# A three-layer graph network and a token FFN on one core: the pace at which gathered sets are added in layers 2 and 3

## The chip, the cores and the metric

The kernel runs on one core of one Trainium2 chip. The metric is the device time of one execution in microseconds (us); lower is better. A core has five engines that run side by side and meet at semaphores: TensorE (PE in the profile; PEld is its weight load), VectorE (DVE), ScalarE (ACT), GpSimd (POOL) and SyncE (SP), which here only issues DMAs.

## The reference, cut to what matters

Inputs: `x` (6250 nodes x 256), 200,000 edges `src -> dst` (sorted by `dst`), three 256x256 weights, and an FFN.

```python
def conv(x, W, b):                      # one layer, with self loops
    h = x @ W
    return segment_sum(h[src] * norm[:, None], dst) + b

h = relu(conv(layernorm(x), W1, b1))
h = relu(conv(h, W2, b2))
x = x + conv(h, W3, b3)
# then a gated FFN on the 3124 nodes with the highest router weight, taken by top_k
```

`norm` is `dinv[src] * dinv[dst]`. So each layer sums, for every node, the rows of its neighbours. The edge count per destination falls with the node's number.

## The kernel before, in words

The 6250 nodes make 49 tiles of 128 rows. The sum over neighbours is done in two ways, both on TensorE:

- **By counts** (tiles 0 to 30, `DENSE = 31`): a dense matrix of edge counts is built once in layer 1, kept in DRAM (`counts`), and multiplied with all source rows (`hl`, each row as a float32r value and its remainder, so 512 columns). A tile takes 49 matmuls. They come in 7 *steps* of 7 matmuls (`add_up`, L735). Each step needs a *piece* of 7 x 128 counts: loaded by SP (`whole`, L932), eight loads ahead, and cast to float32r by `piece_of`, on ACT (L727) or, for the piece numbers in `CASTS`, on DVE (L729): numbers 0 and 3 in layer 2, number 3 in layer 3. Casts run two steps ahead (`AHEAD`).
- **Gathered** (tiles 31 to 48): their edges are cut into 359 *chunks* of 128 edges, two chunks to a *set*, so `SETS` is 180. For a chunk POOL fetches the source rows by an indirect DMA (`fetch`, L600). ACT and DVE split the rows of a set into value and remainder and DVE makes a selection matrix (`halve`, L609 and L619; `rest`, L624). TensorE adds it with two matmuls (`add_set`, L632). A gathered tile ends with one matmul for its own rows (L637). Up to seven sets are fetched ahead (`MSGS`).

In layers 2 and 3 the loop over `order` (L942 to L973) has 217 steps: 14 for tiles 0 and 1, whose pieces alternate, and 7 for each of tiles 2 to 30. In each step `prepare` halves the sets that the *next* step will add and casts the piece for two steps on, `add_up` does the 7 matmuls, and `gathered` adds the sets that are due. How many are due after step k is the list `now["due"]`, made by `pace`:

```python
def pace(n, late):
    return [max(0, SETS * (k + 1 - late)) // (n - late) for k in range(n)] + [SETS] * 2
```

`LATE[1]` is 6. With n = 217 the 180 sets fall on steps 7 to 216, 0 or 1 to a step, so about every seventh step has no set, and the last set of tile 48 is added in step 216, the last step of tile 30.

A finished tile goes through `onward`, which hangs its later work on the ends and starts of later steps (`at_end`, `at_start`), so that it stands in each engine's order among that step's work:

- `total` (DVE, L527 and L528), at the end of the next step. In layers 1 and 2: `turned` (PE transposes, L287), `positive` (ACT, L293), `multiplied` (PE, L298), `sent_on` (ACT, L545, and a DMA to `sent`, L546).
- In layer 3 `total` goes on to `residual` (DVE, L549 to L555), which adds the input row tile. SP loads that tile (`c_xt`, L522) when `onward` is called; for tile 48, which is not full, DVE zeroes it first (L521). Then `rooted` (ACT, L560), `normalised` (DVE, L276 to L281 and L568 to L576) and `summed` (ACT, L581, and DMAs to `c_rows` and `out`, L582 and L583), each at the end of one step later.

PE, DVE, ACT and POOL run in the order written here; the order on SP's queue comes from the scheduler. After the loop `finish` runs what is still hung up. The next layer starts by reading `sent` back (`arrive`, L950 to L952); POOL can gather for it only when all of `sent` has landed. After layer 3 the top-k search begins (L1012 on), and its L1017 waits for the last DMAs out of layer 3's buffers.

Of the kernel before, what the change touches and what calls it, by code (L numbers as in the profile page):

```python
# [56 lines left out]
LATE = [12, 6]  # L57
# [50 lines left out]
def by_counts(  # L108
# [396 lines left out]
    def next_step():  # L505
        run(1)
        steps.append(None)
        run(0)

    def finish():  # L510
        while behind:
            next_step()


    def onward(layer, t, pa):
        xt = None
        if layer == 2:
            n = P if t < NT - 1 else LAST
            xt = later["2"].tile([P, D], FP, name="c_xt2", bufs=4)
            if n < P:  # L520
                nc.vector.memset(xt[96:, :], 0.0)  # L521
            nc.sync.dma_start(xt[:n, :], x[t * P : t * P + n, :])  # L522
        at_end(1, total, layer, t, pa, xt)
# [62 lines left out]
    SETS = ceil(len(CHUNKS) / GB)  # L586
# [64 lines left out]
    def gathered(layer, now, until):  # L651
        for b in range(now["added"], until):
            add_set(layer, b)
        now["added"] = max(now["added"], until)
# [69 lines left out]
    def piece_of(layer, counts_7, i):  # L724
        piece = later["l3"].tile([P, PIECE, P], FR, name="piece")
        if layer is None or i not in CASTS[layer]:
            nc.scalar.activation(piece, counts_7, AF.Copy)  # L727
        else:
            nc.vector.tensor_copy(piece, counts_7)  # L729
        return piece  # L730

    def add_up(pa, piece, i, parts, sources=range(NT // PIECE)):
        for j in parts:
            q = i * PIECE + j
            nc.tensor.matmul(  # L735
                pa, piece[:, j, :], hl[:, q].rearrange("p two d -> p (two d)"),
                start=(i == sources[0] and j == 0), stop=(i == sources[-1] and j == PIECE - 1),
            )

    def new_sums():  # L740
        return ps_a.tile([P, 2 * D], FP, name="c_pa")

    NS = NT // PIECE
    AHEAD = 2

    def pace(n, late):

        return [max(0, SETS * (k + 1 - late)) // (n - late) for k in range(n)] + [SETS] * 2

    def prepare(layer, now, n, order, cast):  # L750

        made = ready(layer, now, now["due"][n + 1]) if n >= LATE[layer > 0] - 5 else []
        if n + AHEAD < len(order):
            cast(n + AHEAD)
        for m in made:
            if m:
                rest(*m)
# [65 lines left out]
    now = {"fetched": 0, "halved": 0, "added": 0}  # L823
# [3 lines left out]
    order = [(t, i) for t in TILES_BY for i in range(NS)]  # L827
# [9 lines left out]
    def cast(n):  # L837
        t, i = order[n]
        pieces[n] = piece_of(0 if n < len(order) - 2 * NS else None, strips[t][:, i * PIECE : (i + 1) * PIECE, :], i)
# [90 lines left out]
    def load(t, i):  # L930
        whole = l8p.tile([P, PIECE, P], F16, name="whole")
        nc.sync.dma_start(  # L932
            whole.rearrange("p h d -> p (h d)"), counts[t][:, i * PIECE * P : (i + 1) * PIECE * P]
        )
        return whole

    with tc.manual_schedule(engines=ordered):
        for layer in (1, 2):
            now = {"fetched": 0, "halved": 0, "added": 0}
            pieces = {}  # L940

            sources = SOURCES[layer - 1]  # L942
            order = [(t, i) for i in sources for t in range(2)]
            order += [(t, i) for t in range(2, DENSE) for i in range(NS)]
            now["due"] = pace(len(order), LATE[1])

            def arrive(i):
                for q in range(i * PIECE, (i + 1) * PIECE):
                    m = l8p.tile([P, D], FP, name="message")
                    nc.sync.dma_start(m, sent[layer][q * P : (q + 1) * P, :])  # L950
                    nc.scalar.activation(hl[:, q, 0, :], m, AF.Copy)
                    nc.vector.tensor_sub(hl[:, q, 1, :], m, hl[:, q, 0, :].bitcast(FP))  # L952

            def cast(n):
                t, i = order[n]
                pieces[n] = piece_of(layer, load(t, i), i)

            for n in range(AHEAD):
                cast(n)
            arrive(sources[0])  # L960
            sums = {}
            for n, (t, i) in enumerate(order):
                prepare(layer, now, n, order, cast)
                by = sources if t < 2 else range(NS)
                if i == by[0]:
                    sums[t] = new_sums()
                if t == 0 and i != sources[-1]:
                    arrive(sources[sources.index(i) + 1])
                add_up(sums[t], pieces.pop(n), i, range(PIECE), by)
                gathered(layer, now, now["due"][n])  # L970
                if i == by[-1]:
                    onward(layer, t, sums.pop(t))
                next_step()  # L973
            finish()
# [727 lines left out]
```

## Time and profile before

| | |
|---|---|
| median of 7 runs | 2401.84 us (2395.0 to 2417.58) |
| the profiled execution: its time | 2402.01 us |
| its span, first to last instruction | 2400.2 us, mean granted TensorE clock 0.931 |
| busy over the span | PE 1995.5, PEld 1498.7, DVE 1367.7, ACT 1207.8, POOL 1251.4 us |
| 943 to 1535 us (layer 2) | PE 524.2, DVE 284.0, ACT 294.3, POOL 361.3 of 592 us |
| 1584 to 2136 us (layer 3 after its start) | PE 457.1, DVE 386.6, ACT 282.7, POOL 335.7 of 552 us |

The profile is one execution. Its times run from the span's start. A line such as `2129.16 4.29 DMA c_xt<-in_x` in the chain of waits says: from 2129.16 us on, for 4.29 us, what came next waited for that transfer. In a timeline the bracket at the end of a line gives the engine's idle time before the instruction and what ended it. Matmul rows overlap, so their weight loads (PEld) show the pace better: seven loads of a step take 1.57 us at full clock.

### The profile page before, as it was taken

The page shows a single profiled execution, that of the slowest core. Times are in us where ns is not written, and L with a number is a line of the kernel's source. Part 1 is how long each engine was busy: PE and PEld are TensorE (multiplying, and loading weights), DVE is VectorE, ACT ScalarE, POOL GpSimd, SP SyncE. Part 2 cuts the span into 40 slices and gives each one's busy share as a digit, 9 for nine tenths or more (in the row PEclk, how much of TensorE's full clock was granted, in tenths as well). Part 3 has the DMA queues.
Part 4 walks back from the last instruction along what each step waited for, and adds up shares of the span by engine and source line. Part 5 has one row for each costly group of instructions (what it writes and reads, how often), then busy time and mean ns, then how long its engine had stood idle before and what let it go on. Part 6 is the DMA issues. An engine that isn't in the chain of part 4 may idle for free.

```text
span 2400.2 us, 30448 instructions
## 1 busy us (share of the span) xinstructions
PE 1995.5 (83%) x9636; PEld 1498.7 (62%) x9636; DVE 1367.7 (57%) x3370; ACT 1207.8 (50%) x1986; POOL 1251.4 (52%) x1228
## 2 busy tenths in 40 slices
PE   4849899989998876888989889888888878845997
PEld 2636666666676655666777677666666656634665
DVE  6475555666677784644444444477676767763111
ACT  2667677655656433644544544565454545431111
POOL 5325666666665501555666566466656656611221
PEclk8859999999999988999999999999999999976999
DMA  6276788787876514865666556587676767731110
GB/s 187 81 256 196 211 250 249 220 246 232 231 234 195 174 52 140 258 182 177 185 176 189 175 178 181 179 266 214 200 211 210 217 202 227 210 103 42 48 54 22
DMA packets 229052, 435.60 MB, mean 181 GB/s; under 512 B 35358, under 2 KB 139092, under 8 KB 224881
## 3 DMA queue, kind: packets, MB, share of 16 engines
q0 software_dynamic: 92992, 205.70, 30.5%
q1 hardware_dynamic: 104357, 192.11, 25.0%
q10 hardware_dynamic: 31532, 35.75, 4.4%
q8 instruction: 78, 1.28, 0.2%
q14 instruction: 93, 0.76, 0.1%
HBM read 335.50 MB, written 99.61 MB: 181 GB/s over the span
## 4 chain that ended last, share of the span: by engine, by line
PE 55%; DVE 17%; issue 8%; ACT 7%; another core or an unknown queue 5%; DMA 3%; POOL 3%; ACTq 1%; SPq 0%; DVEq 0%; POOLq 0%
PE c_pa L735 27%; PE ps_g L632 8%; PE ps_b L689 5%; PE c_ph L1135 4%; PE c_po L1143 4%; PE c_pt L298 4%; DVE half L624 3%; POOL msg L600 3%; ACT strip L705 2%; ACT piece L727 2%; PE ps_x L298 2%; DVE hot_l L669 2%; DVE hot_w L669 2%; ACT half L619 1%
## 5 line engine op out<-in xcount | busy, mean ns | idle before, releaser
L735 PE MATMUL c_pa<-hl,piece 128*128 128x512 f32 x4557 | 1301.2, 418 | 62.7 <-ACT piece L727 25.1
L735 PEld LDWEIGHTS c_pa<-hl,piece 128*128 128x128 f32 x4557 | 855.0, 197 | 247.1 <-issue 44.8
L600 POOL DMA_INDIRECT msg<-sent,source x718 | 722.0, 1006 | 537.3 <-DVE half L624 211.1
L600 POOL DMA_INDIRECT half<-sent,source x359 | 384.3, 1070 | 251.8 <-PE ps_g L632 81.9
L609 DVE TENSOR_TENSOR pick_sel<-up_h,local 128x256 fp32r<-128x256 f16 x540 | 227.4, 421 | 433.9 <-PE ps_g L632 210.9
L632 PE MATMUL ps_g<-half,pick_sel 128*128 128x512 f32 x1077 | 358.7, 412 | 98.4 <-DVE half L624 90.0
L727 ACT ACTIVATE piece<-whole 128x896 fp32r<-128x896 f16 x341 | 320.0, 941 | 157.3 <-remote 58.4
L705 ACT ACTIVATE strip<-ps_b 128x441 f16<-128x441 f32 (+3 forms) x441 | 304.1, 750 | 184.5 <-PE ps_b L689 144.4
L619 ACT ACTIVATE half<-msg 128x512 fp32r<-128x512 f32 x360 | 223.8, 625 | 294.8 <-PE ps_g L632 81.6
L632 PEld LDWEIGHTS ps_g<-half,pick_sel 128*128 128x128 f32 x1077 | 201.5, 194 | 174.6 <-DVE half L624 119.3
L624 DVE TENSOR_TENSOR half<-msg,half 128x512 fp32r<-128x512 f32 x360 | 248.5, 690 | 87.3 <-ACT half L619 48.8
L689 PE MATMUL ps_b<-hot_w,hot_l 128*128 128x98 f16 (+2 forms) x2171 | 213.9, 225 | 96.8 <-DVE hot_l L669 47.1
L689 PEld LDWEIGHTS <-hot_l 128*128 128x128 f16 x2171 | 139.0, 101 | 216.0 <-issue 148.3
L727 ACT ACTIVATE piece<-strip 128x896 fp32r<-128x896 f16 x159 | 150.7, 949 | 99.8 <-PE c_pa L735 78.9
L669 DVE TENSOR_TENSOR hot_w<-up_w,codes 128x1176 f16<-128x1176 f16 (+2 forms) x181 | 165.6, 915 | 61.3 <-PE ps_b L689 46.7
L669 DVE TENSOR_TENSOR hot_l<-up_l,codes 128x1536 f16<-128x1536 f16 x181 | 172.4, 952 | 0.0
L1139 ACT ACTIVATE ht<-c_ph,b_sb 128x512 f32<-128x512 f32 (+2 forms) x64 | 38.0, 594 | 188.4 <-PE c_ph L1135 185.7
L298 PE MATMUL c_pt<-c_wg,c_zt 128*128 128x256 f32 x392 | 102.9, 388 | 6.5 <-ACT c_zt L293 4.7
L1151 POOL DMA_INDIRECT out<-o,pick x25 | 25.2, 1007 | 140.6 <-DVE o L1148 140.6
L1147 DVE TENSOR_TENSOR o<-c_po,b_sb 128x256 f32<-128x256 f32 x25 | 10.6, 425 | 149.2 <-PE c_po L1143 149.2
L1135 PE MATMUL c_ph<-yt,w_sb 128*128 128x512 f32 (+2 forms) x256 | 91.1, 515 | 0.6 <-DVE yt L1130 0.6
L1143 PE MATMUL c_po<-w_sb,ht 128*128 128x256 f32 x400 | 88.5, 381 | 0.0
(218 smaller groups left out, 1561.3 us busy)
## 6 DMA issues: line engine op xcount, KB each, us to landing
whole<-counts SPq DMA_DIRECT2D x434, 224.0 KB
counts<-strip SPq DMA_DIRECT2D x31, 1568.0 KB
c_rows<-ys ACTq DMA_DIRECT2D x49, 256.5 KB
sent<-hl SPq DMA_DIRECT2D x7, 1792.0 KB
sent<-c_h ACTq DMA_DIRECT2D x98, 128.0 KB
message<-sent SPq DMA_DIRECT2D x98, 128.0 KB
msg<-sent,source POOLq DMA_INDIRECT x718
c_xt<-in_x SPq DMA_DIRECT2D x48, 128.0 KB
```

What stands on the lines that cost most here:

```text
L298: nc.tensor.matmul(pt[:, 1, :], zt[:, k, :], w_sb[:, k, :], start=(k == 0), stop=(k == KD - 1))
L600: nc.gpsimd.indirect_dma_start(out=out_j, out_offset=None, in_=sent[layer], in_offset=bass.IndirectOffsetOnAxis(ap=source[:, i : i + 1], a ...
L609: nc.vector.tensor_tensor(pick[:, :n], up_h[:, None, :].to_broadcast([P, n, P]), local[:, b * GB : b * GB + n, None].to_broadcast([P, n, P ...
L619: nc.scalar.activation(half[:, :n, 0, :], msg[:, :n], AF.Copy)
L624: nc.vector.tensor_sub(half[:, :n, 1, :], msg[:, :n], half[:, :n, 0, :].bitcast(FP))
L632: nc.tensor.matmul(open_sums[t], pick[:, j, :], half[:, j].rearrange("p two d -> p (two d)"), start=(k == 0), stop=False)
L669: nc.vector.tensor_tensor(rows_k[:, : n // 2, :cols, :], up[:, None, :cols, :].to_broadcast([P, n // 2, cols, 2]), code.rearrange("p (k tw ...
L689: nc.tensor.matmul(pb[:, at_c : at_c + NT * width], row_l[:, k // 2, :, k % 2], row_w[:, k // 2, : NT * width, k % 2], start=(c == 0), sto ...
L705: nc.scalar.activation(strip[:, :, d0 : d0 + n * width].rearrange("p h (a j) -> p a h j", j=width), pb[:, at_c : at_c + n * NT * width].re ...
L727: nc.scalar.activation(piece, counts_7, AF.Copy)
L735: nc.tensor.matmul(pa, piece[:, j, :], hl[:, q].rearrange("p two d -> p (two d)"), start=(i == sources[0] and j == 0), stop=(i == sources[ ...
L1135: nc.tensor.matmul(ph[:, : n * P], w1_sb[:, k, f * P : (f + 1) * P], yt[:, k, : n * P], start=(k == 0), stop=(k == KD - 1),)
```

## The change

In layers 2 and 3 the pace is computed for 7 steps fewer (`NS` is 7), and the last 7 steps get the full number.

```diff
             order += [(t, i) for t in range(2, DENSE) for i in range(NS)]
-            now["due"] = pace(len(order), LATE[1])
+
+            now["due"] = pace(len(order) - NS, LATE[1]) + [SETS] * NS
```

With n = 210 the 180 sets fall on steps 7 to 209, and steps 210 to 216, which are tile 30, add none. Steps 12 to 210 held 30 steps without a set; now steps 14 to 201 hold 23. Tile 48 ends in step 209, which is also the last step of tile 29. Nothing is added or removed otherwise, and the lines from L946 on move down by one.

## The prediction

> **What bounds the kernel now.** I read the page first, to see which engine carries the span. In the chain that ended last TensorE has the largest share:
>
> ```profile
> PE 55%; DVE 17%; issue 8%; ACT 7%; another core or an unknown queue 5%; DMA 3%; POOL 3%; ACTq 1%; SPq 0%; DVEq 0%; POOLq 0%
> ```
>
> The change moves matmuls within layers 2 and 3 and adds none, so what counts is where TensorE idles there. Second view: PE's waits, for layer 2 (943 to 1541 us) and then layer 3 (1541 to 2140 us); columns: total us, times, longest.
>
> ```profile
> PE ps_g L632 <- DVE half L624: 35.2, 22, 3.7
> ...
> PE ps_g L632 <- DVE half L624: 54.7, 35, 3.9
> PE c_pa L735 <- ACT piece L727: 17.8, 5, 5.8
> ```
>
> The reader is to see that the largest wait is a set's matmuls waiting for their remainder from DVE: 1.6 us each (35.2 / 22, 54.7 / 35), in a layer of 600 us. POOL is not the bound: 361.3 us busy of 592 in layer 2, and its last gather begins at 1517.8, when six more sets are still to be added.
>
> Third view: the ends of the two layers in the chain of waits (start, us, what). First layer 2, where tiles 48 and 30 end together:
>
> ```profile
> 1534.28 1.60 PE c_pa L735 x7
> 1535.88 0.23 PE ps_g L632
> 1536.11 0.25 PE ps_g L637
> 1536.38 0.49 DVE c_z L527
> ...
> 1538.44 0.41 PE c_pt L287 x2
> 1538.86 0.88 PE c_pt L298 x4
> ...
> 1540.69 0.48 ACT c_h L545
> ```
>
> The reader is to see PE end its sums at 1536.36 and the second tile's last ACT operation begin 4.33 us later. Layer 3:
>
> ```profile
> 2128.86 0.28 DVE c_xt L521
> 2129.16 4.29 DMA c_xt<-in_x
> ...
> 2133.55 0.43 DVE c_z L549
> ...
> 2139.35 0.08 DVE c_rstd L276
> ...
> 2141.90 3.35 DMA out<-ys
> ...
> 2145.37 0.15 DVE bits L1017
> ```
>
> Here PE's sums end at 2131.6 (L637 in the timeline). Everything up to 2145.37 is DVE, ACT and DMA for the two tiles, one after the other: 13.8 us in which PE has two matmuls of 1 column. Fourth view, the stretches of the last seven steps (us, then busy us of PE and PEld with counts):
>
> ```profile
> 1520.00:1536.36 16.36, 16.34 (x74) 13.17 (x72) 7.07 (x14) 7.30 (x13) 0.00 (x0) 1.00 0.45 124
> ...
> 2114.50:2131.60 17.10, 14.69 (x63) 11.32 (x61) 12.75 (x47) 8.15 (x14) 0.00 (x0) 1.00 0.15 53
> ```
>
> In layer 2 they have no gap; in layer 3 PE idles 2.4 us, before the set added at 2122.54.
>
> **The change, part by part.** *Units.* A step's seven matmuls take 1.60 us, a set 0.47, a tile's way through L287 and L298 0.22 + 0.87 = 1.09 (rows at 1524.05 and 1524.27 of the same chain). No instruction is added, so the sum starts at 0 and takes only waits and overlap.
>
> *Work moved off the last seven steps.* Six sets and L637 of tile 48 (6 x 0.47 + 0.25 = 3.1 us of PE) stand earlier in each layer. PE does them either way: 0.
>
> *End of layer 2.* Tile 48 now ends in step 209, and its 1.09 us on PE run inside steps 210 to 216 instead of after them: the sums end 1.09 later. Then one tile is left, and its L545 begins 3.16 us after PE's last sum, as at the end of layer 1, where tile 0 ends alone (sum ends 936.63, L545 at 939.79): 4.33 - 3.16 = 1.17 saved. Net **-0.1**. What follows (two casts, the first rows of layer 3, POOL's first gather) hangs on that same store in both. Between -1.2 (if the 1.09 falls into a gap) and +1.1 (if the single tile gains nothing).
>
> *End of layer 3.* One tile alone: from its own rows, L527 (2134.76) to the end of L555 (2137.07) 2.31, the root on ACT and the way back 0.3, L276 to the issue of the last store 2.64 (2139.26 to 2141.90), landing 3.35, L1017 0.1: 8.8 us in place of 13.8, **-5.0**. In this lies the wait for `c_xt` (0.92 us, 2132.63 to 2133.55): tile 30's load no longer stands behind tile 48's zeroing on SP, and is there long before. Nothing else is late next: the search needs this tile's key.
>
> *A new wait, in the last seven steps of layer 3.* Call T the end of PE's step 209. Tiles 48 and 29 now finish there together, and their DVE work stands ahead of casts. DVE, from T: both tiles through L555, 5.45 us with the `c_xt` wait (2131.63 to 2137.07 in the rows above); then the DVE cast for step 213, 0.65 (mean 646 ns in layer 3): ready at T + 6.1. PE, with three bare steps, wants it at T + 4.8: **+1.3**. On ACT the cast for step 216 stands behind both tiles' L581, L582 and L583. In the rows of before, 5.36 us pass from the first L276 (2136.99) to the end of the second L583 (2142.35). The first L276 now follows the DVE cast: 6.1 + 5.36 + 0.95 for the cast is T + 12.4, while PE ends step 215 at 6.1 + 4.8 = T + 10.9: **+1.5**. Queued behind: on ACT only that cast, on DVE nothing that PE wants; no one but PE waits. Bounds: 0, if DVE gets ahead, and +5.4, if no part of DVE's 5.45 us is covered: I take +2.8, because all its rows are from the same two tiles in the same order.
>
> The Trainium skill, page "DMA: Bandwidth & Descriptors", section "Anatomy of one DMA", gives 2.0 us plus bytes / 436e3 for a transfer, fitted on GpSimd's path. For tile 48's 106 KB that is an estimate of 2.25 us against the 4.29 of the row above. By it DVE would not wait, the two gaps would shrink to 1.9 and the total be 0.9 lower; the row decides.
>
> *The gap of before's last steps* (2.4 us at 2122.54): a step without a set can't have it, but the sets now stand elsewhere and can. Between -2.4 and 0; I take **-1.2**, the middle.
>
> *The denser stretch.* Sets per step rise from 180 / 210 to 180 / 203, 3%. POOL needs 2 x 1.25 us a set (0.95 and 0.30 in the timeline), 2.2 us a step where a step takes 2.7 (565 / 210): covered. DMA is 0.62 and 0.69 busy there: covered. What could move are the waits for L624. In layers 2 and 3 PE gaps over 0.3 us from step 19 on sum to 55.3 and 87.4 us. I placed each by its step. In the three steps after a step without a set there are 41.6 and 57.5 us in 87 steps, elsewhere 13.7 and 29.9 in 111: 1.07 and 1.18 us extra per such step. Seven of these steps leave each layer's middle. If they cause the extra, 7 x 2.25 = 15.8 us go. But in many places they coincide with tile ends, whose number stays. From the other side, a step without a set may be the slack that lets DVE catch up: each that is lost then costs one wait of 1.6, 14 x 1.6 = +22. I take 0: the number of sets, tile ends and DVE operations is unchanged, and both ends need the missing steps to be the cause.
>
> Sum: -0.1 - 5.0 + 2.8 - 1.2 = -3.5. The profiled execution took 2402.0 us, 0.2 above the median shown: **2398.5 us**.
>
> One row warns that a gap can cost more than itself:
>
> ```profile
> 2084.28 1.22 PE L632 MATMUL ps_g<-half,pick_sel 128*128 128x512 f32 x2 [2.53 <-DVE half L624]
> ...
> 2084.88 2.75 PEld L735 LDWEIGHTS c_pa<-hl,piece 128*128 128x128 f32 x7
> ...
> 2122.54 0.74 PE L632 MATMUL ps_g<-half,pick_sel 128*128 128x512 f32 x2 [2.40 <-DVE half L624]
> ...
> 2122.89 1.58 PEld L735 LDWEIGHTS c_pa<-hl,piece 128*128 128x128 f32 x7
> ```
>
> After 2.53 us of idling the next step ran at 2.75 us, after 2.40 at full pace. The new gaps of 1.3 and 1.5 are below both, so I charge nothing; merged into one they would cost 1.2 more. The page "TensorE: Matmul & The Clock Gate", section "What's actually happening", puts the drop to half clock after an idle window of about 3.4 us; by it even the merged gap would be free. The row at 2.53 differs and decides.
>
> **Rivals.** *Faster: the steps without a set are the cause of PE's gaps.* For: the extra above, in both layers. Against: in layer 3 the same gaps also gather just ahead of tile ends. 2402.0 - 3.5 - 15.8 = 2383.
>
> *Slower: they were the slack.* DVE is 70% busy in layer 3 (386.6 of 552), and its queue is where sets wait. Place: L624 in the denser stretch; price 1.6 a wait. Two more waits eat the gain, ten more make it slower by 0.5%, all fourteen give 2402.0 - 3.5 + 22 = 2421. Against: there are no more sets, and the 3% is small.
>
> *It doesn't do what it says:* POOL or DVE is late, so that the sets still stop PE inside tile 30. In the built order of PE's instructions no set stands behind step 209, so such lateness would show ahead of step 210, not in it. POOL needs 359 x 1.25 = 449 us and has over 560. Time then about 2402.
>
> **How the numbers follow.** Forecast 0.65, POOL rival 0.05, faster rival 0.18, slower rival 0.12. A change of 0.5% is 12 us, about what a measurement of this kernel can tell from none. The first two cases lie within it: 0.70; faster 0.18; slower 0.12. The range runs halfway and more to the rivals: 2385 to 2411. The forecast's own range is 2393 to 2404, from its bounds.
>
> **What would show it.** After: one tile between PE's last sum and L1017, 8.8 us; two PE gaps in the last seven steps of layer 3, before steps 213 and 216, the first on DVE's L729, the second on ACT's L727; layer 2's L545 3.2 us after the last sum; PE's waits for L624 near 35 and 55 us. I am wrong if these waits move by over 10 us, or if no gap stands in those seven steps.

## The result, and the profile after

The changed kernel takes 2410.97 us (median of 30 runs, 2399.21 to 2422.80), the kernel before 2397.64 us beside it (72 runs). The ratio is 1.0052 with a 95% interval of 1.0039 to 1.0065: 9 to 16 us slower, where -3.5 was forecast. The profiled execution after took 2411.1 us (span 2409.4), before 2402.0 us (span 2400.2). From `L946` on, the line numbers of the changed kernel are one higher.

The chain that ended last, as shares of the span: PE has lost two points and "issue" has gained two.

```profile
PE 53%; DVE 17%; issue 10%; ACT 6%; another core or an unknown queue 5%; POOL 4%; DMA 2%; ACTq 1%; SPq 0%; POOLq 0%; DVEq 0%
```

PE's waits in layers 2 and 3 after (columns: total us, times, longest):

```profile
PE ps_g L632 <- DVE half L624: 44.8, 21, 5.0
...
PE ps_g L632 <- DVE half L624: 59.3, 38, 5.5
PE c_pa L735 <- ACT piece L727: 19.4, 6, 4.3
PE ps_g L632 <- issue: 11.3, 12, 2.6
```

The waits for L624 are as many as before (59 against 57), but longer: 104.1 us against 89.9.

The last seven steps, in the view by stretches (us; busy us of PE, PEld, DVE, ACT and POOL with counts; clock, DMA share, GB/s). Layer 2 has no gap, layer 3 idles 2.5 us:

```profile
1524.30:1537.89 13.59, 13.55 (x62) 10.92 (x60) 2.38 (x5) 4.94 (x8) 0.00 (x0) 1.00 0.41 118
2134.50:2148.70 14.20, 11.74 (x49) 8.69 (x48) 8.78 (x37) 4.71 (x8) 0.00 (x0) 1.00 0.18 62
```

Where, shows PE's timeline of those steps: ahead of step 213 on the DVE cast, ahead of step 216 on the ACT cast.

```profile
2140.53 5.06 PE L735 MATMUL c_pa<-hl,piece 128*128 128x512 f32 x21 [1.23 <-DVE piece L729]
2146.79 1.89 PE L735 MATMUL c_pa<-hl,piece 128*128 128x512 f32 x7 [1.20 <-ACT piece L727]
```

The end of layer 3 in the chain of waits (start, us, what): one tile, its store, the first step of the search.

```profile
2148.71 0.50 DVE c_z L527
...
2151.08 0.21 ACT c_rstd L560
...
2153.94 2.82 DMA out<-ys
...
2156.89 0.15 DVE bits L1018
```

PE's last sum ends at 2148.67, so this takes 8.2 us; it took 13.8. Up to here everything stands as forecast. The loss stands ahead of step 210. The view that shows it gives a tile's operations of one layer in one line, with the start of the first and of the last. For the matmuls of the sets, layers 2 and 3 before:

```profile
L632 PE MATMUL ps_g<-half,pick_sel x359: 389/397/793, 975.0 to 1535.7; 128*128 128x512 f32 x180
...
L632 PE MATMUL ps_g<-half,pick_sel x359: 387/398/797, 1567.6 to 2131.0; 128*128 128x512 f32 x180
```

And after:

```profile
L632 PE MATMUL ps_g<-half,pick_sel x359: 389/397/794, 969.7 to 1523.8; 128*128 128x512 f32 x180
...
L632 PE MATMUL ps_g<-half,pick_sel x359: 389/399/797, 1565.9 to 2133.9; 128*128 128x512 f32 x180
```

From a layer's first set to its last I call the **set span**. Before it is 560.7 and 563.4 us, after 554.1 and 568.0, although after has seven steps less in it, 13.6 and 11.7 us of PE's busy time by the two stretches above. The seven bare steps (steps without a set) then come on top: 13.9 and 14.6 us from the last set to the layer's last sum. So the sets were not brought forward; bare steps were put behind them.

### The profile page after: what moved, and what is told of

Same layout as the page of the kernel before. It is cut to its first block, busy times and chain, and to the rows that moved or that the text cites. A ratio compares the mean times of both kernels' runs of the same rounds, so it can differ in the third digit from the quotient of the medians.

```text
span 2409.4 us, 30424 instructions
## 1 busy us (share of the span) xinstructions
PE 1994.6 (83%) x9636; PEld 1496.4 (62%) x9636; DVE 1367.5 (57%) x3370; ACT 1207.0 (50%) x1986; POOL 1251.4 (52%) x1228
## 4 chain that ended last, share of the span: by engine, by line
PE 53%; DVE 17%; issue 10%; ACT 6%; another core or an unknown queue 5%; POOL 4%; DMA 2%; ACTq 1%; SPq 0%; POOLq 0%; DVEq 0%
PE c_pa L735 26%; PE ps_g L632 8%; PE ps_b L689 4%; POOL msg L600 4%; PE c_ph L1136 4%; PE c_po L1144 4%; PE c_pt L298 3%; DVE half L624 2%; PE ps_x L298 2%; ACT strip L705 2%; DVE hot_w L669 2%; DVE hot_l L669 2%; ACT piece L727 2%; DVE pick_sel L609 1%
## 5 line engine op out<-in xcount | busy, mean ns | idle before, releaser
L632 PE MATMUL ps_g<-half,pick_sel 128*128 128x512 f32 x1077 | 362.7, 416 | 125.9 <-DVE half L624 104.1
L727 ACT ACTIVATE piece<-whole 128x896 fp32r<-128x896 f16 x341 | 319.4, 940 | 123.3 <-remote 36.4
L624 DVE TENSOR_TENSOR half<-msg,half 128x512 fp32r<-128x512 f32 x360 | 248.4, 690 | 92.4 <-ACT half L619 54.0
L1148 DVE TENSOR_TENSOR o<-c_po,b_sb 128x256 f32<-128x256 f32 x25 | 10.6, 425 | 149.2 <-PE c_po L1144 149.2
L729 DVE CAST piece<-whole 128x896 fp32r<-128x896 f16 x93 | 58.6, 631 | 54.6 <-remote 18.1
```

What stands on the lines that cost most here:

```text
L624: nc.vector.tensor_sub(half[:, :n, 1, :], msg[:, :n], half[:, :n, 0, :].bitcast(FP))
L632: nc.tensor.matmul(open_sums[t], pick[:, j, :], half[:, j].rearrange("p two d -> p (two d)"), start=(k == 0), stop=False)
```

## The experiments

The span and the tail are from each run's one profiled execution, times and intervals from all its runs; each is compared with the kernel before on the same chip. The ratio has its own estimate and can differ by one or two thousandths from the quotient of the medians. In the table, "steps with sets" runs from the first set's step to the last's; "span" is the set span of layer 2 / layer 3, "tail" what follows it to the last sum, "end" the time from the last sum of layer 3 to L1017.

| run | steps with sets | median us | ratio to before | span us | tail us | end us |
|---|---|---|---|---|---|---|
| before | 210 | 2397.6 | 1 | 560.7 / 563.4 | 0 / 0 | 13.8 |
| the change | 203 | 2411.0 | 1.0052 [1.0039, 1.0065] | 554.1 / 568.0 | 13.9 / 14.6 | 8.2 |
| `c1_change` | 203 | 2415.8 | 1.0068 [1.0039, 1.0097] | 555.4 / 560.3 | 13.9 / 14.9 | 8.1 |
| `e1_layer2` | 203 / 210 | 2407.6 | 1.0049 [1.0018, 1.0080] | 552.9 / 563.4 | 13.9 / 0 | 14.0 |
| `e2_layer3` | 210 / 203 | 2409.0 | 1.0062 [1.0040, 1.0084] | 561.5 / 559.9 | 0 / 14.9 | 8.2 |
| `e3_head` | 203, late | 2418.9 | 1.0098 [1.0065, 1.0130] | 550.2 / 564.6 | 0 / 0 | 13.3 |
| `e4_two` | 208 | 2414.0 | 1.0067 [1.0031, 1.0103] | 544.8 / 570.7 | 3.7 / 3.7 | 13.2 |
| `x1_dense` | 192, late | 2480.2 | 1.0184 [1.0151, 1.0218] | 554.2 / 566.9 | 0 / 0 | 14.0 |
| `p1_shift` | 211 | 2441.4 | 1.0032 [1.0011, 1.0054] | 569.6 / 592.7 | 0 / 0 | 13.6 |
| `r1_before_3bufs` | 210 | 2425.9 | 0.9964 [0.9943, 0.9986] | 569.8 / 578.3 | 0 / 0 | 14.4 |
| `r2_after_3bufs` | 203 | 2447.2 | 1.0062 [1.0038, 1.0086] | 562.1 / 579.5 | 13.9 / 15.6 | 8.1 |
| `n1_before_nopick` | 210 | 2390.8 | 0.9972 [0.9948, 0.9996] | 551.2 / 561.3 | 0 / 0 | 14.1 |
| `n2_after_nopick` | 203 | 2407.9 | 1.0033 [1.0010, 1.0056] | 549.0 / 559.2 | 13.9 / 14.8 | 8.2 |
| `n3_before_nogather` | 210 | 2230.0 | 0.9301 [0.9272, 0.9329] | 478.6 / 461.5 | 0 / 0 | 13.9 |
| `n4_after_nogather` | 203 | 2220.6 | 0.9263 [0.9238, 0.9288] | 465.6 / 450.9 | 13.9 / 14.8 | 8.1 |
| `c2_plain` | 210 | 2222.7 | 0.9264 [0.9219, 0.9310] | 484.6 / 467.2 | 0 / 0 | 14.0 |
| `s1_before_plain` | 210 | 2166.5 | 1.0003 [0.9987, 1.0019] | 484.8 / 465.3 | 0 / 0 | 13.9 |
| `s2_after_plain` | 203 | 2167.9 | 1.0010 [0.9999, 1.0021] | 471.8 / 459.9 | 13.9 / 14.8 | 8.0 |
| `g1_before_half` | 210 | 2154.2 | 0.9947 [0.9928, 0.9966] | 481.7 / 463.0 | 0 / 0 | 13.9 |
| `g2_after_half` | 203 | 2146.6 | 0.9912 [0.9895, 0.9928] | 467.4 / 455.8 | 13.9 / 14.9 | 8.2 |

The kernel before took 2398.0 us beside the `e` runs, 2430.6 beside `r`, `p1` and `x1`, 2399.1 beside `n`, 2401.7 beside `c`, and 2165.0 us beside `s` and `g`. It was profiled once, in an execution of 2402.0 us. So the spans of `r`, `p1`, `x1`, `s` and `g` are not to be set against its own, but only against those of the same chip. The chip of `s` and `g` comes back below.

### Where the loss is: one layer at a time

`e1_layer2` and `e2_layer3` make the change in one layer only; `e3_head` has its density, with the seven bare steps ahead of the sets and the old shared end; `e4_two` takes two steps instead of seven.

```diff
+            tail = NS if layer == 1 else 0        # e2_layer3: layer == 2
+            now["due"] = pace(len(order) - tail, LATE[1]) + [SETS] * tail
...
+            now["due"] = pace(len(order), LATE[1] + NS)               # e3_head
...
+            now["due"] = pace(len(order) - 2, LATE[1]) + [SETS] * 2   # e4_two
```

> The change in layer 2 alone; layer 3 keeps the old pace. Theory A (the loss is in the stretch that carries the sets, because steps without a set are missing there; +4.5 us of it in layer 2 and +14 in layer 3 in the two profiled executions): layer 2 loses 4.5 and its end gives 0.1 back, so +4 us against before. Theory B (the loss is at the new end of layer 3: its new waits and a colder clock behind them): 0 here. Theory C (every new placing of the sets moves the time by some us either way, whatever the density): anything between -8 and +8, and no sum rule with the run of layer 3 alone beyond these two adding up.

> The change in layer 3 alone. Theory A: +14 in the stretch, -5.0 at the end, +2.8 for the two new waits, so +9 to +12 us against before, most of the whole change's +13. Theory B: all of +13. Theory C: between -8 and +13; together with layer 2 alone +13.

> The same density as the change (180 sets in 204 steps), but the seven steps without sets stand at the front, where the sets begin seven steps later; the old shared end of tiles 48 and 30. Theory A: the stretch's loss of 18 us without the gain at the end of layer 3: +15 to +20 us against before. Theory B: 0, since the old end is back. Theory C: anywhere between -8 and +15, not tied to density.

> Two steps less in place of seven. Tile 48 ends two steps (5.4 us) ahead of tile 30. Theory A: 2/7 of the stretch's 18 us is +5, the end of layer 3 gains 4 to 5, and no cast is left behind tile 48's work: about 0 (-2 to +2). Theory B: -4 to -5, since the new waits do not arise. Theory C: -10 to +8.

Each layer alone is slower, by 4 to 19 and by 10 to 20 us, and with the old end (`e3_head`) the loss is larger, 16 to 31 us. Theory B falls: the new end gains. Theory A's sign and place stand. `e3_head` shows why it is dear: its first set comes 16.2 and 17.3 us later, the span shrinks by 10.5 in layer 2 and not at all in layer 3, and nothing is won at the end. `e4_two` was expected near 0 and lost 7 to 25 us. One part is plain: its end takes 13.2 us, because tile 48's work, with 5.31 us for the load of its row tile, outlasts two steps (3.7 us). Its profiled execution (2404.0 us) is among its fastest, and the span of 544.8 in layer 2 is the lowest of all with all gathers; how its median comes to 2414 stays open.

### Density, queue depth, and the mere place

`x1_dense` leaves 12 steps without a set in place of 30. `p1_shift` has each of the 30 stand 3 or 4 steps earlier; its first set also comes a step earlier, in step 6, so that one more bare step, 213, stands among the sets. The two `r` kernels have three buffers and prepare each set a step earlier.

```diff
+            now["due"] = pace(len(order), LATE[1] + 18)                       # x1_dense
...
+            m = len(order) - LATE[1]                                          # p1_shift
+            now["due"] = [max(0, SETS * (k + 1 - LATE[1]) + m // 2) // m for k in range(len(order))]
+            now["due"] = [min(SETS, d) if k >= LATE[1] else 0 for k, d in enumerate(now["due"])] + [SETS] * 2
...
-        pick = later["l3"].tile([P, GB, P], FR, name="pick_sel", bufs=2)
+        pick = later["l3"].tile([P, GB, P], FR, name="pick_sel", bufs=3)      # r1, r2
-        half = later["2"].tile([P, GB, 2, D], FR, name="half", bufs=2)
+        half = later["2"].tile([P, GB, 2, D], FR, name="half", bufs=3)
-        made = ready(layer, now, now["due"][n + 1]) if n >= LATE[layer > 0] - 5 else []
+        made = ready(layer, now, now["due"][n + (1 if layer == 0 else 2)]) if n >= LATE[layer > 0] - 5 else []
```

> 180 sets in steps 24 to 216: twelve steps without a set per layer in place of 30, old shared end. Theory A, at the 18 us that 14 missing steps cost: 36 missing steps make +40 to +60 us against before. The faster rival of the prediction (each step without a set causes 1.1 us of gaps): -40. Theory C: between 0 and +25, not growing with density.

> The kernel before with its own density of sets, but each step without a set 3 or 4 steps earlier in layers 2 and 3 (the first at step 9 in place of 12). Theory A: 0 us against before (-4 to +4), since no such step is missing. Theory C (the place of a step without a set against a tile's end decides): 5 to 20 us slower, because the kernel before would be at the favourable place.

> The kernel before with a third buffer for half and pick_sel and each set prepared one step earlier in layers 2 and 3 (nothing left out). Theory A (sets wait for DVE's remainder because DVE's queue runs late behind tile ends and only two buffers cover it): the waits for L624, 36 and 55 us in the two layers, fall by more than half, and the time by 20 to 60 us. Theory C (only the placing of the sets against tile ends counts, and queue depth does not): within 10 us of before. Theory D (the waits come from PE's own late releases of ACT and DVE): within 10 us of before, waits for L624 as long as they were.

> The changed kernel with the same third buffers and earlier preparation. Theory A: with DVE's queue covered, the missing steps without a set cost nothing, and what is left of the change is the gain at the end of layer 3 and its two new waits: -5 to +2 us against the kernel before with third buffers. Theory C and theory D: +10 to +16 against it, as without the third buffers.

`x1_dense` loses 37 to 53 us, about what theory A said, but most of it elsewhere. Its sets of layer 3:

```profile
L632 PE MATMUL ps_g<-half,pick_sel x359: 389/398/796, 1642.7 to 2209.7; 128*128 128x512 f32 x180
```

567.0 us, in 192 steps, in which PE has 18 steps x 1.60 = 29 us less to do than before. The sets come at 3.17 us each (567.0 / 179). Before it was 3.15 (563.4 / 179), but in an execution of 2402.0 us, and on this chip before takes 2430.6. What is lost is the head: the first set stands 62.8 and 57.8 us after the start of the layer, 26.4 and 23.4 before, 70.8 us later in all. As only 37 to 53 us were lost, the two spans may have shrunk by 18 to 34 us (an estimate from these numbers), of the 58 that PE saves.

The queue in front of the sets is not the cause. With third buffers PE hardly waits for L624 in layer 3 (0.5 us, once), but now 74.6 us for the casts, for which it waited 17.8 us before; before's two rows together were 72.5.

```profile
PE c_pa L735 <- ACT piece L727: 74.6, 27, 8.9
```

The change on top of third buffers costs 21 us (2447.2 against 2425.9; the intervals in the table do not meet). So theory A fails where it says why, and with it the slower rival's mechanism. `p1_shift`, 2.7 to 13 us slower at nearly the same density, says that the place of the bare steps counts too (theory C); by how much each, these runs do not tell. (Its profiled execution, 2454.9 us, was the slowest of its 12, so its spans are on the long side; so are those of `r1_before_3bufs`, whose profiled execution took 2435.9.) `r1_before_3bufs`, 3 to 14 us faster than before, is the one version that beats before and still computes what the reference does.

### Whose work: DVE's, or the gathers

`n1`, `n2`: `pick_sel` is made for two sets of each layer and used again. `n3`, `n4`: seven sets are gathered in each layer and used again.

```diff
+        pick = kept.get((layer, b % 2)) if layer else None     # n1, n2
+        if pick is None:
...
+            if b >= MSGS[layer]:                                # n3, n4
+                messages[b] = kept[layer, b % MSGS[layer]]
+                return
```

> The kernel before, and in layers 2 and 3 the one-hot pick_sel is made for the first two sets only and used again by all others (so DVE has 178 operations of 0.42 us less in each layer; what is summed is not the reference's). Theory M1 (DVE's work is the limit in the stretch): PE's gaps go with it, 30 to 80 us less than before. Theory M2 (gathers and loads, that is DMA and GpSimd, are the limit) and theory M3 (PE's late releases of ACT and DVE are, whatever these have to do): less than 15 us.

> The changed kernel with the same left out. Theory M1: with DVE relieved the denser stretch costs nothing, so -6 to +3 us against the kernel before with the same left out. Theories M2 and M3: +8 to +16 against it, as in the full kernels.

> The kernel before, and in layers 2 and 3 only the first seven sets are gathered and used again by all others (no later gather on GpSimd, a third of the DMA traffic less; what is summed is not the reference's). Theory M2: 30 to 80 us less than before. Theories M1 and M3: less than 15 us.

> The changed kernel with the same gathers left out. Theory M2: -6 to +3 us against the kernel before with the same left out. Theories M1 and M3: +8 to +16 against it.

Taking 178 x 0.42 = 75 us of DVE's work out of each layer gives 1 to 12 us, and the change still costs 17 us on top: M1 falls. Taking the gathers out gives 169 us, far more than expected, and turns the change round: -9.4 us by the medians (ratio of n4 to n3 0.996, 0.993 to 0.999 by resampling their six runs each). The two layers themselves say -0.7: the spans shrink by 13.0 and 10.6, the tails add 13.9 and 14.8, the end gives 5.8 back; the profiled pair also differs by 10 us in layer 1, where nothing is changed. Without gathers the span shrinks by nearly what the seven steps take, as the prediction took for granted.

### The gathers' bytes, or GpSimd's issuing

Each gather becomes a plain load of 128 whole rows on SP's queue (`s1`, `c2` before; `s2` after), or every second set is left ungathered (`g1`, `g2`).

```diff
+            if layer:                                                    # s1, s2, c2
+                q = i % NT
+                nc.sync.dma_start(out_j, sent[layer][q * P : (q + 1) * P, :])
+                continue
...
+            if b >= MSGS[layer] and b % 2:                               # g1, g2
+                messages[b] = kept[layer]
+                return
```

> The kernel before, and in layers 2 and 3 each gather on GpSimd is replaced by a plain load of 128 whole rows on SP's queue (the same bytes into the same buffers; what is summed is not the reference's). Theory G (while GpSimd issues gathers, PE's releases reach ACT and DVE late): as without gathers, 2225 to 2270 us. Theory T (the gathers' bytes take the DMA engines from the other loads): 2360 to 2400 us.

> The changed kernel with the same replacement. Theory G: -10 to -3 us against the kernel before with the same replacement. Theory T: +8 to +16 against it.

> The kernel before, and in layers 2 and 3 every second set from the seventh on takes its messages from one constant buffer, so that half the gathers are left out (what is summed is not the reference's). Theory G: the cost follows the number of gathers, about half of the 169 us: 2300 to 2330 us. If GpSimd has to be nearly always busy for the cost to arise: 2230 to 2260. Theory T: half as well, 2300 to 2330.

> The changed kernel with the same half of the gathers left out. Theories G and T: halfway between +13 and -9, so -4 to +6 us against the kernel before with the same left out; if GpSimd has to be nearly always busy for the cost to arise: -10 to -5.

These four met a chip on which the kernel before itself took 2165.0 us (23 runs). There the gathers cost little to begin with (plain loads 1.0003, 0.9987 to 1.0019; half the gathers left out 0.9947, 0.9928 to 0.9966), so G and T were not told apart. They do show the change where sets are not held up: +1.4 us with plain loads (the two intervals overlap), -7.6 with half the gathers (the intervals just touch). Two kernels were run again, on the chip of the `n` runs.

> The changed kernel once more, nothing else. Theory H (the denser stretch costs time only where PE's releases come late while GpSimd issues gathers): where the kernel before runs near 2165 us, -10 to -2 us against it; where it runs near 2400, +9 to +16. If the denser stretch costs time in itself, +9 to +16 in both.

> The kernel before with each gather of layers 2 and 3 replaced by a plain load of the same bytes on SP's queue, once more. Where the kernel before runs near 2400 us, theory G (GpSimd's issuing makes the releases late): 2225 to 2270; theory T (the gathers' bytes do): 2360 to 2400. Where it runs near 2165, both: 2160 to 2172.

Here before takes 2401.7 us. The change costs 9 to 23 us again, and plain loads of the same bytes take 179 us off, a little more than G said. So it is not the bytes as such. But a plain load differs from a gather in more than the engine that issues it: it reads rows that lie side by side, and it stands in SP's queue. The runs do not separate these. The sets of layer 3 with plain loads:

```profile
L636 PE MATMUL ps_g<-half,pick_sel x359: 389/397/783, 1489.2 to 1956.4; 128*128 128x512 f32 x180
```

467.2 us, 96 less than before, at the same steps and the same sets.

### What the gathers do: late releases

The timeline of all engines of before, around one of PE's longest gaps (start, us, engine, line, in brackets the idle time before and its end):

```profile
1686.34 0.63 PE L632 MATMUL ps_g<-half,pick_sel 128*128 128x512 f32 x2
...
1688.91 0.95 POOL L600 DMA_INDIRECT msg<-sent,source  x1 [0.30 <-issue]
1691.78 0.95 ACT L727 ACTIVATE piece<-whole 128x896 fp32r<-128x896 f16 x1 [6.62 <-remote]
1691.83 0.43 DVE L609 TENSOR_TENSOR pick_sel<-up_h,local 128x256 fp32r<-128x256 f16 x1 [5.94 <-remote]
...
1692.78 2.08 PE L735 MATMUL c_pa<-hl,piece 128*128 128x512 f32 x4 [5.81 <-ACT piece L727]
```

ACT and DVE both wait for PE's semaphore. PE's set ends by the record at 1686.97, yet both start at 1691.8, 4.8 us later; PE, out of casts, idles 5.81. "remote" means that an update of the awaited semaphore is on record at the end of the wait, here of PE's at 1691.80, but that no instruction that makes one ended in the 1.5 us before it. With plain loads, the same hand-over:

```profile
1707.66 0.63 PE L636 MATMUL ps_g<-half,pick_sel 128*128 128x512 f32 x2
...
1708.33 0.63 ACT L623 ACTIVATE half<-msg 128x512 fp32r<-128x512 f32 x1 [0.59 <-PE ps_g L636]
1708.33 0.43 DVE L613 TENSOR_TENSOR pick_sel<-up_h,local 128x256 fp32r<-128x256 f16 x1 [0.71 <-PE ps_g L636]
```

The set ends at 1708.29, and both start 0.04 us later. How much there is of it, the waits of ACT and DVE in layers 2 and 3 of before tell (total us, times, longest; the largest rows):

```profile
ACT half L619 <- remote: 65.5, 21, 7.3
ACT piece L727 <- remote: 58.4, 14, 7.1
...
DVE pick_sel L609 <- remote: 90.6, 23, 8.2
```

The changed kernel has 88.1, 36.4 and 120.5 in these rows; `c2_plain` has not one such wait in the two layers, nor have `s1_before_plain` and `g1_before_half`. These totals count the whole wait, of which lateness is a part. The trace's own record of semaphore updates gives that part. In all 70 "remote" waits of before the semaphore is PE's, and its update stands 1.5 to 4.8 us behind the end of the last PE instruction that makes one. By the same count 185 of before's 307 waits of ACT and DVE on PE's semaphore in the two layers ended over 0.2 us late. In `c2_plain` all 417 ended within 0.02 us, while in its layer 1 (from 200 to 880 us), which gathers as ever, 60 of 402 came over 0.2 us late, up to 2.1.

So, everywhere but on the chip of `s` and `g`, a set passes from PE to ACT and DVE and back to PE late while GpSimd gathers, and neither third buffers nor less work for DVE gains more than 14 us. GpSimd was not short of time itself: in before it waits 211.1 us in layers 2 and 3 for DVE to free a buffer. That PE's releases get through when GpSimd pauses would explain a set span that hardly moves. It fits the trace of before: away from the ends of the two layers, 43 of 81 releases over 1 us late came when GpSimd's last gather had ended over 1 us earlier, which holds for an eighth of the time. But a late release also makes GpSimd wait, by way of DVE, so this is not shown. Nor is the record without gaps: before has 540 updates of PE's semaphore in the two layers for 780 instructions that make one, `c2_plain` 780 for 780. That the recording itself takes part in the delay is not excluded.

The Trainium skill, page "Perfetto Trace Analysis", section "Tensor Engine Instruction (MATMUL, LD_WEIGHTS)", says that a matmul's end is estimated and that its semaphore is raised only when PSUM has acknowledged all bytes. The record's end is thus no proof of the release; the 0.02 us with plain loads shows that the estimate is good when nothing holds the release up. The page "DMA: Bandwidth & Descriptors", section "SWDGE vs HWDGE vs iDMA", says that GpSimd builds descriptors for its DMAs in rings in SBUF, and that loads from SP or ACT never touch these. That fits what separates `c2_plain` from before, but no run here shows what in it holds PE's releases.

## Why the prediction was wrong, step by step

- **Work moved off the last seven steps, 0.** The matmuls are the same (9636 on PE in both). What was silently counted is that the stretch with the sets becomes shorter by the time of the seven steps that leave it. This is the step that failed; it stands under "the denser stretch" below.
- **End of layer 2, -0.1: right.** L545 begins 3.34 us after the last sum (forecast 3.16, before 4.33).
- **End of layer 3, -5.0: right**, 8.22 us against 13.78. The forecast's terms add up to 8.7 (not 8.8); the half us below that is the store's landing, 2.82 instead of 3.35. In the 20 profiled executions it is 8.0 to 8.2 where tile 48 ends seven steps ahead (8 of them), and 13.2 to 14.4 in the others.
- **The new wait, +2.8: right**, 1.23 and 1.20 us at the steps and engines named; the last seven steps took 14.2 us (by the forecast 7 x 1.60 + 2.8 = 14.0). That the gaps cost no clock held too: 1.00 is granted over the seven steps.
- **The gap of before's last steps, -1.2:** it isn't in those steps any more; whether it went or moved can't be told from the other gaps.
- **The denser stretch, 0: wrong.** "The number of sets, tile ends and DVE operations is unchanged" was true and beside the point. The spans of the three profiled executions of the change in layer 2 (554.1, 555.4, 552.9) lie 7.0 below the two of before's pace (560.7, 561.5), those in layer 3 (568.0, 560.3, 559.9) 0.7 below (563.4, 563.4), where 13.9 and 14.6 to 14.9 us of bare steps were added behind. That is +6.9 and +14.1; with -5.7 for the end of layer 3 and -1.0 for that of layer 2, +14.3. Measured: +13.3 and +14.1. These are single executions, on different chips where before takes 2398 to 2402 us, and the three of layer 3 differ by 8 us among themselves. The sign that the prediction named, waits for L624 that move by over 10 us, came only in the sum of the two layers (+14.2; 9.6 and 4.6 each).
- **"POOL: covered; DMA: covered".** GpSimd had pauses, but its gathers hold up others all the same. The trace of before did show it: 243 us of "remote" waits of ACT and DVE in the two layers, all on PE's semaphore. The prediction read PE's waits only, and did not follow them to what ended DVE's and ACT's own.
- **The faster rival** (bare steps cause the gaps) fell: with 18 fewer of them in each layer `x1_dense` was the slowest. Its price rests on how the gaps are placed: by the step of the matmul that ends each gap, 33.5 and 60.6 us stand in the three steps after a bare one, where the prediction has 41.6 and 57.5, and the price is 13.5 us in place of 15.8. **The slower rival** had the place and nearly the size (2421), for another reason: not 1.6 us of waiting for each missing step (there are 59 waits for L624, not 71), but a span that does not shrink. **"Doesn't do what it says"** fell: no set stands behind step 209.

Where its premise holds, the forecast of -3.5 is near: in layers without held-up releases the change comes to between -9.4 and +1.4 us in three pairs.

## What to carry to other kernels

Before work is packed into fewer steps, take the time from its first to its last piece, divide by the pieces, and ask what sets that rate; if it isn't the engine whose steps are saved, the steps come back behind it at their full price. A wait for an engine is not explained until the wait of that engine is: follow it until a wait ends on something that the record shows. A rival that forecasts the loss for a wrong reason can still be worth more range than the reason deserves.

## What the runs showed of the hardware

- While GpSimd issues indirect gathers, PE's semaphore can reach ACT and DVE late, where before takes 2398 to 2431 us: 4.8 us in the place shown, 1.5 to 4.8 us in 70 waits of before's two layers. With plain loads of the same bytes on SP's queue no such wait is over 0.02 us late, and 179 us of 2402 go with them.
- On one chip the same kernel took 2165.0 us, 10% less, with a granted clock of 0.957 against 0.92 to 0.94. No late release shows in the kernels profiled there, not even in layer 1 of `s1_before_plain`, which gathers as before does, and plain loads gain nothing (1.0003, 0.9987 to 1.0019). What makes the difference between the chips, and what the change does there with all its gathers, was not measured.
